# Relational graph layer with normalization on one core: base products read two chunks later, node sums three, masks made two chunks ahead

## The chip, the core and the metric

The kernel runs on one core of a Trainium2 chip. The core has five engines that run their own instruction streams and meet through semaphores: TensorE (matrix products, "PE" in the profile, with its weight loads as "PEld"), VectorE ("DVE"), ScalarE ("ACT"), GpSimd ("POOL") and SyncE ("SP"). Products of TensorE land in PSUM, which VectorE and ScalarE read; everything else lives in SBUF, and DMA queues move data between SBUF and device memory. The metric is the device time of one execution in microseconds (us); less is better.

## The reference

There are 50,000 nodes with 128 features, 850,000 edges sorted by their destination (400,000 in both directions and one from each node to itself), and 16 relations whose 128x128 matrices are mixtures of 8 bases. Two layers run one after the other, then a residual and a normalization of each node's row:

```python
def _rgcn_layer(h, src, dst, rel, basis, w_comp, loop_w, bias):
    W = jnp.einsum('rb,bio->rio', w_comp, basis)
    seg = dst.astype(jnp.int32) * N_REL + rel.astype(jnp.int32)
    agg = jax.ops.segment_sum(h[src], seg, num_segments=N_ENT * N_REL)
    agg = agg.reshape(N_ENT, N_REL, -1)
    msg = jnp.einsum('nri,rio->no', agg, W)
    out = msg + h @ loop_w + bias
    return jax.nn.relu(out)
...
x = _layernorm(x + _L0_gnn_ref(x, ...), axis=-1)
```

## The kernel before

**Chunks.** The 800,000 edges that are not from a node to itself are cut into 625 chunks (C) of 10 tiles (K) of 128 edges. Since the edges are sorted by destination, a tile touches few nodes; the kernel lets a tile touch at most 12 (WN). A chunk therefore has 120 "slots", 12 to a tile. Both layers go through all chunks, so there are 1,250 passes of the loop over `c`, fully unrolled.

**One chunk.** GpSimd gathers the source rows, one indirect DMA for each tile (`gather`, L198), into one of GATHERS = 6 buffers, in an order that is two chunks (FETCH) ahead in its own stream. VectorE makes the mask `hot` (L789): for each edge, base and slot, the weight of the edge's relation in that base, or 0. Ten products `pa` (L837, five in each half) sum the gathered rows by base and slot; ScalarE copies each half to `aT` (L844). `slots` multiplies `aT` by the eight bases (`ps`, L689, eight products into one sum), and ScalarE copies the result (L693). `nodes_of` puts slots at their nodes: a 0/1 mask `own` (L699) times the slots, and, because a node's edges can run over a chunk's end, a second mask `shift` (L706) times the last chunk's result `kept`, moved by the distance between the two chunks' first nodes; both products go into `pn` (L703, L707). VectorE adds what the node has from itself (`a`, L709), ScalarE copies `pn` to `kept` (L712), and the row is finished and stored.

**Edges from a node to itself** do not go through chunks. `from_itself` takes a block of 128 nodes: load (L656), transpose on TensorE into `po` (L205), copy to `hT` (L207), two products `hb` with four bases each (L667), each weighed by VectorE into `by` (L670), one product with the loop weights (L678), its bias (L679), a sum over nine parts (L681), and a store to `L` (L682). Every eighth block also needs `loop_weights` (L642, L646). 391 blocks in a layer go with 625 chunks, about 62 blocks for 100 chunks.

**Order.** The orders of TensorE and GpSimd are those in which the program is written (`manual_schedule`); those of the other engines are left to the framework's scheduler. TensorE works through its instructions in order, so one that waits holds up all that follow. In pass `c` its order is: `pn` of chunk c-2, transpose of the block, `pa` first half, `hb` first, `ps` of chunk c-1, `hb` second, `pa` second half, the block's loop product, and every fourth chunk the relation weights `pm` (L615). The mask for chunk c+1 is made at the end of the pass.

**PSUM.** It has eight banks, and each has a user: `fixed` (constants and scratch of VectorE), two for `pa`, one for `po` (transposes, loop products, set-up), one for `ps`, one for `pn`, one for `pm`, one for `hb`.

Of the kernel before, what the change touches and what calls it, by code (L numbers as in the profile page):

```python
# [48 lines left out]
P = 128  # L50
EPR = 850000
ROW = 10
WN = 12
# [13 lines left out]
GATHERS = 6  # L67
# [9 lines left out]
def tile_rgcn_resnorm(  # L77
# [57 lines left out]
    grid, apart = fixed[:, 0, :], fixed[:, 1, :]  # L135
    nc.vector.tensor_copy(grid, col)
    nc.vector.tensor_scalar(apart, col, -1.0, part, op0=OP.mult, op1=OP.add)
# [57 lines left out]
    ps_h = ctx.enter_context(tc.tile_pool(name="ps_h", bufs=1, space=PSUM))  # L195
# [22 lines left out]

    base_i = consts.tile([1, C], I32, name="base_i")
    dist = consts.tile([P, C], F32, name="dist")  # L220
    slot = consts.tile([P, C], F32, name="slot")
    first_of = consts.tile([1, C], F32, name="first_of")
# [6 lines left out]
    picked = consts.tile([P, 5 * NG + len(ROWS) + 3], F32, name="picked")  # L229
    ones = consts.tile([P, max(LIVE, C)], F32, name="ones")  # L230
    place = consts.tile([P, RUN], F32, name="place")
    place64 = consts.tile([P, LIVE], F32, name="place64")
# [12 lines left out]
    nc.gpsimd.iota(place64, pattern=[[64, LIVE]], base=0, channel_multiplier=0, allow_small_or_imprecise_dtypes=True)  # L245
# [190 lines left out]
    def rows_of(j, pool):  # L436
# [44 lines left out]
        if (r0 + m) * LIVE > M:  # L481
            last = pool.tile([P, 1], F32, name="last")
            nc.vector.tensor_scalar(
                last, part, -64.0 * LIVE, 64.0 * (M - 1 - r0 * LIVE), op0=OP.mult, op1=OP.add
            )
            nc.vector.scalar_tensor_tensor(
                keyf[:m], place64[:m], last[:m], keyf[:m], op0=OP.subtract, op1=OP.max
            )
        rel8 = pool.tile([P, LIVE], U8, name="rel8")
# [27 lines left out]
        nc.vector.tensor_copy(dist[:, a:b], po[:, : b - a])  # L517
# [13 lines left out]
    def count_up(pool):  # L531
# [22 lines left out]
        nc.vector.tensor_scalar(picked[0:1, last + 2 :], first_of[:, 0:1], 0.0, None, op0=OP.is_equal)  # L554
# [8 lines left out]
            off[:, 1:2], total[:1, 1:2], float(E + 2 * NG * (P + 1) + 2 * C + 1), None, op0=OP.not_equal  # L563
# [19 lines left out]
    def chunked():  # L583
        with (
# [3 lines left out]
        ):  # L588

# [34 lines left out]
            def loop_weights(i, n):  # L624
# [15 lines left out]
                po = ps_o.tile([P, D], F32, name="po")  # L640
# [8 lines left out]
            def from_itself(i, of, n, lws):  # L649
# [11 lines left out]
                hT = turned(h[:m], m, sb)  # L661
                by = sb.tile([P, NB + 1, D], F32, name="by", bufs=1)
                few = BANK // D
                for b in range(0, NB, few):
                    yield
                    hb = ps_h.tile([P, BANK], F32, name="hb")
                    nc.tensor.matmul(  # L667
                        hb[:m], hT, BASIS[n][:, b : b + few, :].rearrange("p b d -> p (b d)"), start=True, stop=True
                    )
                    nc.vector.tensor_tensor(  # L670
                        by[:m, b : b + few, :],
                        hb[:m].rearrange("p (b d) -> p b d", d=D),
                        lw[:m, b : b + few, None].to_broadcast([m, few, D]),
                        op=OP.mult,
                    )
                yield
                po = ps_o.tile([P, D], F32, name="po")
# [7 lines left out]
            def slots(c, k, aT, n):  # L685

                ps = ps_n.tile([P, D], F32, name="ps")
# [4 lines left out]
                st = sb.tile([P, D], F32, name="slots")  # L692
# [3 lines left out]
            def nodes_of(kept, c, k, st, n0, ls, xw, n):  # L696

                own = sb.tile([P, P], F32, name="own")
                nc.vector.tensor_scalar(  # L699
                    own[: k * WN], grid[: k * WN, :P], slot[: k * WN, c : c + 1], None, op0=OP.is_equal  # L700
                )
                pn = ps_n.tile([P, D], F32, name="pn")
                nc.tensor.matmul(pn, own[: k * WN], st[: k * WN], start=True, stop=not c)  # L703
                if c:
                    shift = sb.tile([P, P], F32, name="shift")
                    nc.vector.tensor_scalar(shift, apart, dist[:, c - 1 : c], None, op0=OP.is_equal)  # L706
                    nc.tensor.matmul(pn, shift, kept, start=False, stop=True)  # L707
                a = sb.tile([P, D], F32, name="a")
                nc.vector.tensor_add(a, pn, ls)  # L709
                if c < C - 1:  # L710
                    kept = sb.tile([P, D], F32, name="kept")
                    nc.scalar.copy(kept, pn)  # L712
# [8 lines left out]
                return kept  # L721
# [48 lines left out]
            for n, of in enumerate((x, H1)):  # L770

                kept, summed_up, multiplied, lws = None, None, None, []
                base, ks = [at(0), None, None], lambda c: min(K, -(-M // P) - c * K)
                own_parts = []
# [5 lines left out]
                def hot_of(c, pm):  # L780
# [7 lines left out]
                    hot = hp.tile([P, K, NB, WN], F32, name="hot")  # L788
# [8 lines left out]
                def loaded(n0):  # L797

                    ls = sb.tile([P, D], F32, name="ls_of")
# [5 lines left out]
                    return ls, xw  # L805
# [3 lines left out]
                for c in range(C):  # L809
                    now[0] = c  # L810
                    if n == 0 and c:

                        next(coming, None)
                        while ready[0] + 1 < len(ROWS) and 2 * min(C, c + FETCH + 4) > ROWS[ready[0] + 1]:
                            next(coming)
                    if c:
                        base = [at(c)] + base[:2]
# [4 lines left out]
                    if c == 0:  # L822
# [3 lines left out]
                        hot = hot_of(c, pm)  # L826
                    if c > 1:
                        kept = nodes_of(kept, c - 2, ks(c - 2), summed_up, base[2], *others, n)
                        others = loaded(base[1])
                    parts = own_parts[0] if own_parts else iter(())  # L830
                    next(parts, None)
                    aT = hp.tile([P, NB, S], F32, name="aT")
                    for k in range(0, ks(c), PER):
# [14 lines left out]
                        if k == 0:  # L848
                            next(parts, None)
                            if c:  # L850
                                summed_up = slots(c - 1, ks(c - 1), multiplied, n)
                            next(parts, None)
                    multiplied = aT
                    for parts in own_parts:
                        done(parts)
                    if c == 1:
                        others = loaded(base[1])
                    if c + 1 < C:
                        if (c + 1) % Q == 0:
                            pm = next(weigh)  # L860
                        hot = hot_of(c + 1, pm)
                        if c + 2 < C and (c + 2) % Q == 0:
                            weigh = weights(c + 2, n)
                            next(weigh)
                        own_parts = []
                        for i in own_nodes(c + 1):
                            own_parts.append(from_itself(i, of, n, lws))
                            if len(own_parts) == 1:
                                next(own_parts[0])
# [5 lines left out]
                last = loaded(base[0])  # L875
                kept = nodes_of(kept, C - 2, ks(C - 2), summed_up, base[1], *others, n)
                summed_up = slots(C - 1, ks(C - 1), multiplied, n)
                nodes_of(kept, C - 1, ks(C - 1), summed_up, base[0], *last, n)
            ordered.close()

    def summed():
        L1 = dram.tile([N, D], F32, name="L1")
        L2 = dram.tile([N, D], F32, name="L2")
        with tc.tile_pool(name="io", bufs=2) as io, tc.tile_pool(name="sbf", bufs=2) as sb:
# [28 lines left out]
            def looped(h, n, L, m, n0):  # L913

                op = ps_n.tile([P, D], F32, name="pn")
# [30 lines left out]
            def added(h, n, L):  # L946


                def block(r0, p):
# [13 lines left out]
                    for e in range(ROW):  # L963
# [35 lines left out]
                        op = ps_n.tile([P, D], F32, name="pn")  # L999
# [68 lines left out]
```

## Time and profile before

| | |
|---|---|
| median of 3 runs (lowest to highest) | 18,924.72 us (18,904.69 to 18,941.53) |
| the profiled execution | 18,936.72 us |
| its span, first to last instruction | 18,934.8 us |
| mean granted TensorE clock | 0.72 |
| busy: TensorE / its weight loads | 10,703.0 / 9,174.1 us |
| busy: VectorE / ScalarE / GpSimd | 6,595.5 / 2,775.4 / 11,864.7 us |
| the span over 1,250 chunks | 15.1 us |

A row of the profile names line, engine and operation, what is written and read, how often, busy time, the mean of one in ns, and the idle time of the engine just before, with what ended most of it. "issue" means that nothing which the profile shows was waited for, and "remote" that the semaphore came but its sender could not be told. The ends of matrix products are modelled, not observed; when a product is really done is seen by when its reader, waiting for it, begins. An indirect DMA on GpSimd is shown for the time in which its descriptors are made, and its data come later.

### The profile page before, as it was taken

How to read it: one execution, taken by the hardware profiler on the slowest of the kernel's cores; microseconds unless marked ns; L12 is line 12 of the kernel's file. 1: busy time of each engine (PE TensorE's matmuls, PEld its weight loads, DVE VectorE, ACT ScalarE, POOL GpSimd, SP SyncE). 2: the span in 40 equal slices, each digit the busy share in tenths (PEclk: the TensorE clock that was granted, in tenths of full speed). 3: DMA queues.
4: the chain of work that ended last, by engine and by line, in shares of the span. 5: the costliest groups of instructions: out<-in, count | busy, mean ns of one | idle time of the engine just before them, and what ended most of it. 6: DMA issues, size and time to landing. Idle time of an engine off the chain costs nothing.

```text
span 18934.8 us, 187693 instructions
## 1 busy us (share of the span) xinstructions
PE 10703.0 (57%) x59198; PEld 9174.1 (48%) x59198; DVE 6595.5 (35%) x14269; ACT 2775.4 (15%) x7815; POOL 11864.7 (63%) x12533
## 2 busy tenths in 40 slices
PE   4555555555555555555555555555555555555555
PEld 3444445444544445445445555445454444444445
DVE  4333334333333332333223333333333333333333
ACT  1111111111111111111111111111111111111111
POOL 5666666665666666666656666666666666666665
PEclk7777777676777776777767777777777777777777
DMA  2222222222222222222222222222222222222222
GB/s 80 69 69 65 68 66 66 66 66 63 62 62 61 61 61 61 61 61 61 61 55 66 67 66 67 66 66 67 65 66 66 66 66 66 65 66 66 66 65 62
DMA packets 1164943, 1227.02 MB, mean 65 GB/s; under 512 B 283055, under 2 KB 952401, under 8 KB 1163937
## 3 DMA queue, kind: packets, MB, share of 16 engines
q0 software_dynamic: 403552, 826.82, 16.8%
q1 hardware_dynamic: 757169, 386.65, 7.1%
q8 instruction: 472, 7.73, 0.2%
q14 instruction: 534, 4.37, 0.1%
q10 hardware_dynamic: 3216, 1.45, 0.0%
HBM read 1059.55 MB, written 154.23 MB: 64 GB/s over the span
## 4 chain that ended last, share of the span: by engine, by line
another core or an unknown queue 22%; PE 17%; issue 7%; DVE 5%; ACT 2%; DMA 0%; POOL 0%; SPq 0%; ACTq 0%; DVEq 0%; POOLq 0%
PE pa L837 6%; PE ps L689 4%; PE hb L667 4%; DVE ls L681 1%; DVE by L670 1%; DVE hot L789 1%; PE pn L703 1%; ACT aT L844 1%; PE pn L707 1%; PE po L678 0%; PE po L205 0%; DVE by L679 0%; ACT slots L693 0%; ACT sd L574 0%
## 5 line engine op out<-in xcount | busy, mean ns | idle before, releaser
L198 POOL DMA_INDIRECT g<-H,src x6250 | 5910.6, 946 | 3393.7 <-issue 1422.2
L198 POOL DMA_INDIRECT g<-in_x_dram,src x6250 | 5927.4, 948 | 3338.4 <-issue 1411.5
L837 PE MATMUL pa<-hot,g 128*128 128x96 f32 x25000 | 4125.3, 326 | 1898.8 <-DVE hot L789 1388.2
L837 PEld LDWEIGHTS pa<-hot,g 128*128 128x128 f32 x25000 | 4014.2, 243 | 2402.1 <-DVE hot L789 1434.6
L689 PEld LDWEIGHTS ps<-basis,aT 128*120 128x120 f32 x20000 | 3222.4, 240 | 927.1 <-issue 849.3
L667 PE MATMUL hb<-basis,hT 128*128 128x512 f32 x3128 | 2273.3, 818 | 2107.1 <-ACT hT L207 915.7
L689 PE MATMUL ps<-basis,aT 128*120 128x128 f32 x20000 | 3211.3, 329 | 224.3 <-issue 150.5
L670 DVE TENSOR_TENSOR by<-hb,lw 128x512 f32<-128x512 f32 x1564 | 1080.1, 691 | 6152.1 <-remote 2557.6
L789 DVE TENSOR_TENSOR hot<-pm,own 128x960 f32<-128x960 f32 x1250 | 1432.6, 1153 | 4113.1 <-remote 3585.2
L844 ACT COPY aT<-pa 128x480 f32<-128x480 f32 x2500 | 1395.2, 558 | 6619.3 <-remote 3577.7
L703 PE MATMUL pn<-slots,own 120*128 120x128 f32 x2500 | 708.5, 373 | 2448.5 <-ACT slots L693 1502.1
L703 PEld LDWEIGHTS pn<-slots,own 120*128 120x128 f32 x2500 | 470.3, 235 | 2593.2 <-ACT slots L693 1583.3
L667 PEld LDWEIGHTS hb<-basis,hT 128*128 128x128 f32 x3128 | 638.1, 253 | 2191.4 <-ACT hT L207 943.1
L681 DVE TENSOR_REDUCE ls<-by 128x128 f32<-128x1152 f32 (+1 forms) x782 | 1656.9, 2119 | 12.1
L693 ACT COPY slots<-ps 120x128 f32<-120x128 f32 x1250 | 332.4, 266 | 5771.4 <-remote 3733.1
L205 PE MATMUL po<-ident,h_own 128*128 128x128 f32 (+1 forms) x782 | 295.8, 378 | 1151.9 <-issue 399.5
L205 PEld LDWEIGHTS po<-ident,h_own 128*128 128x128 f32 (+1 forms) x782 | 138.1, 177 | 1219.9 <-issue 415.1
L707 PE MATMUL pn<-kept,shift 128*128 128x128 f32 x2496 | 604.8, 332 | 12.1 <-DVE shift L706 6.3
L615 PE MATMUL pm<-each,is_rel 128*128 128x64 f32 x3140 | 438.6, 281 | 114.4 <-issue 110.4
L707 PEld LDWEIGHTS pn<-kept,shift 128*128 128x128 f32 x2496 | 493.7, 245 | 14.2 <-DVE shift L706 7.7
L712 ACT COPY kept<-pn 128x128 f32<-128x128 f32 x1248 | 336.1, 269 | 1079.7 <-DVE a L709 603.5
L709 DVE TENSOR_TENSOR a<-pn,ls_of 128x128 f32<-128x128 f32 x1250 | 355.1, 284 | 386.6 <-remote 133.1
(148 smaller groups left out, 5082.0 us busy)
## 6 DMA issues: line engine op xcount, KB each, us to landing
g<-in_x_dram,src POOLq DMA_INDIRECT x6250
g<-H,src POOLq DMA_INDIRECT x6250
ls_of<-L SPq DMA_DIRECT2D x1250, 64.0 KB
L<-ls SPq DMA_DIRECT2D x780, 64.0 KB
H<-h SPq DMA_DIRECT2D x625, 64.0 KB
xw<-in_x_dram SPq DMA_DIRECT2D x625, 64.0 KB
out_dram<-o SPq DMA_DIRECT2D x625, 64.0 KB
h_own<-in_x_dram SPq DMA_DIRECT2D x390, 64.0 KB
```

Of the source, the lines that this page charges most:

```text
L198: nc.gpsimd.indirect_dma_start(out=to, out_offset=None, in_=of, in_offset=bass.IndirectOffsetOnAxis(ap=idx, axis=0))
L205: nc.tensor.transpose(tp[:, :m], h, ident[:m, :m])
L615: nc.tensor.matmul(of[:, :, j * NB : (j + 1) * NB], is_rel[:m, j * P : (j + 1) * P], EACH[n][:m], start=True, stop=True,)
L667: nc.tensor.matmul(hb[:m], hT, BASIS[n][:, b : b + few, :].rearrange("p b d -> p (b d)"), start=True, stop=True)
L670: nc.vector.tensor_tensor(by[:m, b : b + few, :], hb[:m].rearrange("p (b d) -> p b d", d=D), lw[:m, b : b + few, None].to_broadcast([m, fe ...
L681: nc.vector.tensor_reduce(ls[:m], by[:m].rearrange("p b d -> p d b"), AX.X, OP.add)
L689: nc.tensor.matmul(ps[: k * WN], aT[:, b, : k * WN], BASIS[n][:, b, :], start=b == 0, stop=b == NB - 1)
L703: nc.tensor.matmul(pn, own[: k * WN], st[: k * WN], start=True, stop=not c)
L707: nc.tensor.matmul(pn, shift, kept, start=False, stop=True)
L789: nc.vector.tensor_tensor(hot[:, : ks(c)], pm[:, c % Q * K : c % Q * K + ks(c), :, None].to_broadcast([P, ks(c), NB, WN]), own[:, : ks(c), ...
L837: nc.tensor.matmul(pa[:, i * NB * WN : (i + 1) * NB * WN], g[:, k + i, :], hot[:, k + i].rearrange("e b w -> e (b w)"), start=True, stop=True,
L844: nc.scalar.copy(aT[:, :, k * WN : (k + m) * WN].rearrange("d b (i w) -> d i b w", w=WN), pa[:, : m * NB * WN].rearrange("d (i b w) -> d i ...
```

## The change

- **Node sums lie three chunks back** and nothing is kept from chunk to chunk. `pn` of chunk c-3 is made at the end of pass `c` from two slot results: its own, and that of the chunk before it, placed by a second mask of the same kind (`next_slot`). `shift`, `apart`, `dist`, `kept` and its copy go. The slot results have 5 buffers.
- **Bases lie two chunks back**: `ps` of chunk c-2 is made in pass `c`; `aT` has 3 buffers.
- **Masks are made two chunks ahead**: `hot` of chunk c+2 at the end of pass `c`, with 3 buffers.
- **A node block spreads over two passes**: its transpose at the start of pass `c`, its `hb` products and loop product in pass c+1, in the places in which they stood in pass `c`. Its rows are loaded two chunks ahead.
- **PSUM**: `hb` gets two banks. To pay for it, `ps`, `pn`, the loop product and the loop weights become four quarters of one tile, `sums`, that is allocated once and fills one bank; transposes keep `po`.
- **Gather buffers**: 5 for 6.
- A few counts that guard the assumptions change with it.

```diff
-GATHERS = 6
+GATHERS = 5
...
-    ps_h = ctx.enter_context(tc.tile_pool(name="ps_h", bufs=1, space=PSUM))
+    ps_h = ctx.enter_context(tc.tile_pool(name="ps_h", bufs=2, space=PSUM))
+
+    sums = ps_n.tile([P, BANK // P, P], F32, name="sums")
...
-        nc.vector.tensor_copy(dist[:, a:b], po[:, : b - a])
+        nc.vector.tensor_tensor(next_slot[:S, a:b], slot[:S, a:b], po[:S, : b - a], op=OP.subtract)
...
-                po = ps_o.tile([P, D], F32, name="po")
+                po = sums[:, 3, :]
                 for h in range(2):
                     nc.tensor.matmul(
                         po[:, : AT * NB], is_rel[:m, h, :], EACH[n][:m], start=h == 0, stop=h == 1
...
                 hT = turned(h[:m], m, sb)
+                yield
                 by = sb.tile([P, NB + 1, D], F32, name="by", bufs=1)
                 few = BANK // D
                 for b in range(0, NB, few):
-                    yield
                     hb = ps_h.tile([P, BANK], F32, name="hb")
...
-                yield
-                po = ps_o.tile([P, D], F32, name="po")
+                    yield
+                po = sums[:, 2, :]
                 nc.tensor.matmul(po[:m], hT, LOOP[n], start=True, stop=True)
                 nc.vector.tensor_add(by[:m, NB, :], po[:m], BIAS[n][:m])
...
-                ps = ps_n.tile([P, D], F32, name="ps")
+                ps = sums[:, 0, :]
...
-                st = sb.tile([P, D], F32, name="slots")
+                st = sb.tile([P, D], F32, name="slots", bufs=5)
...
-                pn = ps_n.tile([P, D], F32, name="pn")
-                nc.tensor.matmul(pn, own[: k * WN], st[: k * WN], start=True, stop=not c)
-                if c:
-                    shift = sb.tile([P, P], F32, name="shift")
-                    nc.vector.tensor_scalar(shift, apart, dist[:, c - 1 : c], None, op0=OP.is_equal)
-                    nc.tensor.matmul(pn, shift, kept, start=False, stop=True)
+                looked = [(c, slot[:, c : c + 1])]
                 if c:
+                    looked.append((c - 1, next_slot[:, c - 1 : c]))
...
+                pn = sums[:, 1, :]
+                for j, (i, at_node) in enumerate(looked):
+                    k = ks(i) * WN
+                    own = sb.tile([P, P], F32, name=f"own{j % 2}")
+                    nc.vector.tensor_scalar(own[:k], grid[:k, :P], at_node[:k], None, op0=OP.is_equal)
+                    nc.tensor.matmul(pn, own[:k], st[i][:k], start=j == 0, stop=j == len(looked) - 1)
                 a = sb.tile([P, D], F32, name="a")
                 nc.vector.tensor_add(a, pn, ls)
-                if c < C - 1:
-                    kept = sb.tile([P, D], F32, name="kept")
-                    nc.scalar.copy(kept, pn)
...
                     if c > 1:
-                        kept = nodes_of(kept, c - 2, ks(c - 2), summed_up, base[2], *others, n)
-                        others = loaded(base[1])
-                    parts = own_parts[0] if own_parts else iter(())
-                    next(parts, None)
-                    aT = hp.tile([P, NB, S], F32, name="aT")
+                        loaded(c - 2)
+
+                    own, one = coming_own.pop(c, []), iter(())
+                    if len(own) == 1:
+                        one = own[0]
+                        next(one, None)
+                    hot = hots.pop(c)
+                    aT = aTs[c] = hp.tile([P, NB, S], F32, name="aT", bufs=3)
...
                         if k == 0:
-                            next(parts, None)
-                            if c:
-                                summed_up = slots(c - 1, ks(c - 1), multiplied, n)
-                            next(parts, None)
+                            next(staged, None)
+                            if c > 1:
+                                sum_up(c - 2)
...
-                    for parts in own_parts:
-                        done(parts)
...
+                    done(staged)
...
+                    staged = one
+                    if c > 2:
+                        finish(c - 3)
+                    if c + 2 < C:
+                        if (c + 2) % Q == 0:
                             pm = next(weigh)
-                        hot = hot_of(c + 1, pm)
...
+                        hots[c + 2] = hot_of(c + 2, pm)
...
+                    for to in [c + 1] if c == 0 else [2, 3] if c == 1 else [c + 2]:
+                        if to < C:
+                            coming_own[to] = [from_itself(i, of, n, lws) for i in own_nodes(to)]
```

Here `sum_up(c)` calls `slots`, and `finish(c)` calls `nodes_of`. In pass `c` TensorE's order is now: transpose of this chunk's block, `pa` first half, first `hb` of the last chunk's block, `ps` of chunk c-2, `pa` second half, second `hb`, the loop product, `pn` of chunk c-3, and every fourth chunk `pm`.

## The prediction

> **What bounds the kernel now.** First the busy shares: no engine is full, GpSimd is busiest. Then its rows among the costliest groups, the first two lines below: 12,500 gathers of 0.947 us, 11,838 us in all, with 6,732 us idle before them. The list of GpSimd's waits splits that idle time.
>
> ```profile
> PE 10703.0 (57%) x59198; PEld 9174.1 (48%) x59198; DVE 6595.5 (35%) x14269; ACT 2775.4 (15%) x7815; POOL 11864.7 (63%) x12533
> ...
> L198 POOL DMA_INDIRECT g<-H,src x6250 | 5910.6, 946 | 3393.7 <-issue 1422.2
> L198 POOL DMA_INDIRECT g<-in_x_dram,src x6250 | 5927.4, 948 | 3338.4 <-issue 1411.5
> ```
> ```profile
> POOL g L198 <- issue: 2833.6, 9114, 5.8
> POOL g L198 <- PE pa L837: 1621.8, 1277, 33.9
> POOL g L198 <- remote: 1586.1, 1153, 8.9
> ```
>
> The 9,114 short gaps are 0.31 us, GpSimd's own rhythm (0.30 in the timeline). So the gathers cannot take less than 11,838 + 12,500 x 0.30 = 15,588 us. What is left, 6,732 - 3,750 = 2,982 us, is GpSimd standing, mostly for `pa`: a buffer is free when TensorE has used it. The last 365 us of the 18,935 are start, tail and the rest. In the trace's starts of gathers, 1,671 runs are parted by over 1.4 us between starts: 1.34 stops for each of 1,250 chunks, 2,982 / 1,671 = 1.78 us each.
>
> Why does GpSimd stand, if TensorE is 57% busy? The timeline of one chunk answers:
>
> ```profile
> 14066.53 0.56 ACT L844 COPY aT<-pa 128x480 f32<-128x480 f32 x1 [7.26 <-issue]
> 14066.53 1.16 DVE L789 TENSOR_TENSOR hot<-pm,own 128x960 f32<-128x960 f32 x1 [9.76 <-issue]
> ...
> 14069.14 0.94 POOL L198 DMA_INDIRECT g<-H,src  x1 [0.30 <-issue]
> 14070.73 0.35 DVE L699 TENSOR_SCALAR own<-fixed,slot 120x128 f32<-120x128 f32 x1 [2.64 <-remote]
> 14072.83 0.35 DVE L706 TENSOR_SCALAR shift<-fixed,dist 128x128 f32<-128x128 f32 x1 [1.75 <-remote]
> ...
> 14072.86 0.27 ACT L207 COPY hT<-po 128x128 f32<-128x128 f32 x1 [5.78 <-remote]
> 14073.13 0.56 ACT L844 COPY aT<-pa 128x480 f32<-128x480 f32 x1
> 14073.14 0.94 POOL L198 DMA_INDIRECT g<-H,src  x1 [3.06 <-remote]
> 14073.18 0.50 PEld L667 LDWEIGHTS hb<-basis,hT 128*128 128x128 f32 x2 [10.78 <-ACT hT L207]
> ```
>
> The transpose behind that `hT` has its modelled end at 14,060.56, its reader starts at 14,072.86. The products were issued and done by the model, but word of them came 10 us late, and then for all at once, 2 to 3 us after GpSimd had stopped. That is the rule over the whole trace: of TensorE's recorded semaphore updates, some 0.5 a microsecond come within 1.3 us of a gather's start, 10.5 in the slice 3.0 to 3.25 us after the last one. In the first 4 us after gathers resume, readers of `aT` mostly begin 0.1 us after their product; later in a run they take 4 to 12 us. So the kernel beats: GpSimd runs about a chunk of gathers, its credits run out, it stops, word of the products comes, TensorE gets on, credits flow. **The time is 12.47 us of gathers a chunk plus its stops**, and what counts is how far TensorE can issue without word of its own products: each `pa` issued before a stop is a credit at the stop.
>
> TensorE's waits show where it stands:
>
> ```profile
> PE pn L703 <- ACT slots L693: 1502.1, 357, 22.5
> PE pa L837 <- DVE hot L789: 1388.2, 177, 42.4
> PE hb L667 <- ACT hT L207: 915.7, 126, 12.2
> ...
> PE hb L667 <- DVE by L670: 515.7, 86, 29.3
> ...
> PE po L205 <- DVE by L679: 329.2, 135, 13.4
> ```
>
> **What the distances remove.** In their groups with "issue" and the rest, these cost: `pn` 2,448 us, `pa` 1,899, `hb` 2,107, the transpose 1,152; 7,606 us or 6.1 us a chunk. After the change `pn` reads slots of the pass before, `pa` a mask a pass old, `hb` a transpose of the pass before and has two banks; the transpose's bank is no longer the loop product's. All four waits as they stand lose their cause.
>
> **What it leaves alone.** `own` for `shift` is the same on VectorE (339 for 337 ns) and on TensorE (a second `pn` product of 373 ns for one of 332; 1,248 x 2 instructions x 0.041 = 102 us of busy time on an engine with 8,200 idle). The copy to `kept` (336 us of ScalarE's 2,775) goes, hidden and worth nothing while ScalarE is 15% busy. Masks, loads and stores are the same in number. Five buffers for six: GpSimd ends a chunk's gathers a median 70 us, 4.6 chunks, before they are used; one chunk less leaves 55, which hides a landing. The cover is gone only where gathers are held up for longer than that; single waits of over 55 us are few (TensorE's longest are 42.7 us for `hot` and 62.5 without a cause shown). Nothing, with 100 us as the other end. Guards and set-up: under 5 us. Each layer's tail has two more sums behind the last `pa`, some 5 us each with their readers, 20 us in all; layer 2's first gather waits behind it (37.2 us once now).
>
> **SP.** `h_own` is loaded a chunk earlier into three buffers, so its wait for the old transpose (5,486 us at L656 now, `remote`, `pa` and `po` together) stands a chunk nearer to the transpose that frees it, and behind it in SP's queue stand loads of `ls_of` and stores of rows. `ls_of` has a whole chunk to land before `a` needs it. Between nothing and 1 us a chunk if `a` is late; I take nothing.
>
> **What it adds: one bank for four.** `ps`, `pn`, the loop product and the loop weights are now quarters of `sums`. If quarters count as independent there is no new wait. The row for that is the old `po` bank: where transposes and loop products used the same bytes, TensorE waited for L679 (1,152 us with its neighbours). No row shows two users of different bytes in one bank. Here a rule of the Trainium skill speaks against the change: "PSUM — Partial Sum Buffer", section "PSUM bank collisions raise a hardware error", says that an engine may not read a bank while TensorE writes to it, even in other columns, and that one has to guard by bank, not by address. A framework that follows it makes TensorE's every write to `sums` wait for all earlier readers of the bank. In the new order these are three waits:
> - `ps` behind `a` (pn of the pass before), at a distance of a transpose, five `pa` and one `hb`. Nearest row: `hb` behind `hT`, at five `pa`: (2,107 - 516) / 780 = 2.0 us. A further `hb` lies between, but VectorE may be in its 2.1 us sum (L681): 1.75 us a chunk.
> - the loop product behind the copy of `ps`, at five `pa` and one `hb`. Rows: `hb` behind `by` at sixteen `ps` instructions, 516 / 780 = 0.66, and 2.0 as above: 1.3 us, for 62% of chunks 0.8.
> - `pn` behind L679, with nothing between. Row: the transpose behind L679, 1.47 us with `pn` between (0.8 us): 2.3 us for 62%, 1.4; in the other chunks `pn` behind the copy of `ps`, 2.0 for 38%, 0.7.
>
> By the row the added wait is 0; by the rule 1.75 + 0.8 + 2.1 = 4.7 us of the 6.1 come back. I take the rule. More important is where they come back: the wait that parts one beat from the next, slots' copy between `ps` and the next product, was in front of `pn` and is now in front of the loop product, at the same distance. So by the rule TensorE gains no second chunk between stops.
>
> **The sum.** What still goes are stops in mid-chunk. Two waits, `hT` and `by`, stood between the halves of `pa`, so that a stop often found only half a chunk issued; now one, for `a`, stands there. Of the 0.34 stops a chunk beyond one I leave a third, 0.11 (both ends: none, and all 0.34). 1,250 x 1.10 x 1.78 = 2,450 us of standing for 2,982: 530 us less, 20 of it back in the tails, and 18,935 becomes some 18,420. The profiled execution took 18,936.7 us, 2 more than its span and 12 more than the median of the runs, so **18,410 us**, 2.7% faster. With none or all of the 0.34 left: 18,180 to 18,930.
>
> **Rivals.**
> - A, **the distances work in full**: quarters are independent, or the waits on the bank fall into the prompt stretch. TensorE then issues 1.5 to 2 chunks between stops: 1,250 / 1.75 x 1.78 = 1,270 us of standing, 17,220 us. For it: `aT` readers in the first 4 us of a run take 0.1 us. Against: the rule, and `pn` directly behind L679.
> - B, **slower: `pn` behind L679**. The loop product is now the last thing before `pn`, and word of it comes behind five `pa` and one `hb`[...]. Where that falls late in a run of gathers, TensorE stands before the next chunk's first `pa`, and a stop frees nothing new: another stop of 1.78 us. It outweighs the gain from 298 of the 780 blocks on (530 / 1.78); at 60% of them it costs 833 us: 19,240. For it: late in a run readers wait 4 to 12 us. Against: the loop product is released at the stop itself and should be done in the 4 prompt us.
> - C, **nothing changes**: the beat is set by gathers and word of products alone, one stop and a third as before; 18,930.
>
> **Numbers.** My forecast has 0.40, A 0.18, B 0.34, C 0.08. Within 0.2% is what a measurement of this kernel can tell from no change (its three runs span 0.2%): faster 0.57, same 0.07, slower 0.36. The forecast's own range is 18,180 to 18,750. The range for eight in ten reaches to A's 17,220 and past B's 19,240: 17,150 to 19,500.
>
> **What would show it.** Right: `pn` no longer waits for slots, `pa` not for `hot`, `hb` not for `hT`; instead `ps` waits for `a`, the loop product for slots, `pn` for L679; runs of gathers between stops grow from 7.5 to about 9. A is right if those bank waits are missing and runs reach 15 or more. B is right if `pn` stands for L679 over 1,500 us and runs shorten. The prediction is wrong at its root if the stops vanish and TensorE's products still report late, or if readers take no 10 us even in long runs: then gathers do not hold up the reports.

## The result and the profile after

The changed kernel takes 18,726.98 us, median of four runs (18,704.36 to 18,737.19), beside 18,923.88 for the kernel before, measured with it: a ratio of **0.9895, interval 0.9877 to 0.9912**. It is faster, as forecast, but by 1.05% and not by 2.7%. The profiled execution's span is 18,735.4 us, 199.4 less than before.

First the page after: its busy shares, and the rows of the gathers and of the three users of the shared bank `sums` (instructions | busy, mean ns | idle before, what ended most of it).

```profile
PE 11303.9 (60%) x59202; PEld 9682.0 (52%) x59202; DVE 6635.0 (35%) x14275; ACT 2537.0 (14%) x6567; POOL 11856.0 (63%) x12532
...
L200 POOL DMA_INDIRECT g<-in_x_dram,src x6250 | 5919.9, 947 | 3352.7 <-issue 1428.9
L200 POOL DMA_INDIRECT g<-H,src x6250 | 5910.7, 946 | 3346.0 <-issue 1439.6
...
L731 PE MATMUL sums<-slots,own 120*128 120x128 f32 x5000 | 1327.9, 412 | 4360.9 <-DVE by L702 1356.0
...
L712 PE MATMUL sums<-basis,aT 128*120 128x128 f32 x20000 | 3241.2, 330 | 729.6 <-issue 514.2
...
L701 PE MATMUL sums<-loop,hT 128*128 128x128 f32 x1564 | 438.5, 370 | 1613.4 <-ACT slots L716 1275.2
```

The gathers' idle time has hardly moved: 6,698.7 us for 6,732. So most of the 199 us did not come from the stops that the prediction counted. TensorE's waits (us in total, times, longest) have changed places as it said:

```profile
PE sums L731 <- DVE by L702: 1356.0, 455, 23.7
PE sums L701 <- ACT slots L716: 1275.2, 330, 18.3
PE sums L731 <- issue: 1268.8, 240, 16.3
PE sums L731 <- ACT slots L716: 1230.3, 248, 26.7
PE sums L712 <- issue: 514.2, 216, 25.1
...
PE sums L712 <- DVE a L733: 184.9, 84, 7.4
```

The wait of `pa` for `hot` is gone, and that of `hb` for `hT` is down from 915.7 us to 47.9. In their place `pn` (L731) stands for L702, which only shares its bank, and the loop product (L701) for the copy of `ps`. One such place in the timeline (start, duration, engine, instruction, idle before):

```profile
14003.53 0.49 PE L701 MATMUL sums<-loop,hT 128*128 128x128 f32 x2 [1.34 <-ACT slots L716]
14004.50 0.94 POOL L200 DMA_INDIRECT g<-H,src  x1 [0.30 <-issue]
...
14011.20 0.94 POOL L200 DMA_INDIRECT g<-H,src  x1 [0.78 <-remote]
...
14014.47 0.29 DVE L702 TENSOR_TENSOR by<-sums,bias 128x128 f32<-128x128 f32 x1 [0.69 <-remote]
...
14014.82 1.22 PE L731 MATMUL sums<-slots,own 120*128 120x128 f32 x4 [10.80 <-DVE by L702]
...
14016.04 2.29 PE L866 MATMUL pa<-hot,g 128*128 128x96 f32 x10
...
14016.90 0.94 POOL L200 DMA_INDIRECT g<-H,src  x1 [4.75 <-PE pa L866]
```

The loop product goes out at 14,003.53, its reader L702 begins 11 us later, 2.3 us after GpSimd's last gather ended. Then `pn` and ten `pa` go out within 4 us and GpSimd is let on. The beat of before is still there.

The place also shows a firmer sign of a wait than the label in the list: L731 starts 0.06 us after L702 has ended (14,014.47 + 0.29). I counted by that sign: an idle stretch of TensorE "ends on a reader" if TensorE starts again 35 to 75 ns after an instruction of VectorE or ScalarE has ended. Of the 7,411 us for which TensorE stands idle in this trace, 7,044 end on a reader (before: 7,951 of 8,212). L731 alone stands 2,981 us for L702, in 770 places; the list gives 1,356 to it and puts much of the rest down to "issue" or to other engines.

**Where the 199 us came from.** I took every gap between the starts of two gathers above 1.4 us and split off those in which GpSimd does something else in between. It does so 19 times, all in layer 1: it stores parts of the index tables for later chunks (`FULL`, `LREL`), which VectorE prepares bit by bit between its other work. The stores stand at fixed places among the gathers, and GpSimd waits there until VectorE has the input. Their rows among GpSimd's instructions, before:

```profile
L428 POOL DMA_INDIRECT LREL<-l_rel,l_to x10 | 12.2, 1216 | 93.6 <-DVE l_rel L420 72.9 <-DVE loops L337 20.4 <-issue 0.3
L372 POOL DMA_INDIRECT FULL<-full,to_i x10 | 11.5, 1150 | 201.8 <-DVE shift L706 103.2 <-DVE full L370 56.3 <-DVE own L699 42.3
```

and after:

```profile
L374 POOL DMA_INDIRECT FULL<-full,to_i x10 | 11.5, 1149 | 119.1 <-DVE full L372 119.1
L430 POOL DMA_INDIRECT LREL<-l_rel,l_to x10 | 11.5, 1145 | 21.8 <-DVE l_rel L422 19.3 <-issue 2.1 <-DMA g<-in_x_dram,src 0.3
```

The idle time before these twenty (the first lies ahead of all gathers) fell from 295.4 us to 140.9. The whole account, over the rhythm of 1.2485 us from gather to gather (the gap between the layers counts as a stop):

```
                                     before   after
stops between two gathers, number     1,652   1,558
  their time, us                      2,939   2,898     -41
19 gaps that hold a table store, us     294     141    -153
rhythm, start, end, us               15,702  15,696      -6
```

Three quarters of the gain lie in a place that the prediction did not look at, and the stops it was about gave 41 us.

### The profile page after: what moved, and what is told of

Same layout as the page of the kernel before. It is cut to its first block, busy times and chain, and to the rows that moved or that the text cites. A ratio compares the mean times of both kernels' runs of the same rounds, so it can differ in the third digit from the quotient of the medians.

```text
span 18735.4 us, 188402 instructions
## 1 busy us (share of the span) xinstructions
PE 11303.9 (60%) x59202; PEld 9682.0 (52%) x59202; DVE 6635.0 (35%) x14275; ACT 2537.0 (14%) x6567; POOL 11856.0 (63%) x12532
## 5 line engine op out<-in xcount | busy, mean ns | idle before, releaser
L731 PE MATMUL sums<-slots,own 120*128 120x128 f32 x5000 | 1327.9, 412 | 4360.9 <-DVE by L702 1356.0
L712 PEld LDWEIGHTS sums<-basis,aT 128*120 128x120 f32 x20000 | 3188.5, 240 | 1451.3 <-issue 1107.4
L712 PE MATMUL sums<-basis,aT 128*120 128x128 f32 x20000 | 3241.2, 330 | 729.6 <-issue 514.2
L731 PEld LDWEIGHTS sums<-slots,own 120*128 120x128 f32 x5000 | 1008.6, 283 | 4601.1 <-DVE by L702 1468.7
L701 PEld LDWEIGHTS sums<-loop,hT 128*128 128x128 f32 x1564 | 314.8, 234 | 2197.9 <-ACT slots L716 1592.9
L701 PE MATMUL sums<-loop,hT 128*128 128x128 f32 x1564 | 438.5, 370 | 1613.4 <-ACT slots L716 1275.2
L716 ACT COPY slots<-sums 120x128 f32<-120x128 f32 x1250 | 330.7, 265 | 5238.2 <-remote 3725.7
L733 DVE TENSOR_TENSOR a<-sums,ls_of 128x128 f32<-128x128 f32 x1250 | 356.3, 285 | 1532.0 <-remote 442.7
L730 DVE TENSOR_SCALAR own<-fixed,slot 120x128 f32<-120x128 f32 x1250 | 425.5, 340 | 1160.4 <-PE sums L731 740.0
L638 PEld LDWEIGHTS pm<-each,is_rel 128*128 128x128 f32 x3140 | 615.9, 294 | 3.5 <-DVE is_rel L633 3.3
```

Source lines behind the costliest of these rows:

```text
L638: nc.tensor.matmul(of[:, :, j * NB : (j + 1) * NB], is_rel[:m, j * P : (j + 1) * P], EACH[n][:m], start=True, stop=True,)
L701: nc.tensor.matmul(po[:m], hT, LOOP[n], start=True, stop=True)
L712: nc.tensor.matmul(ps[: k * WN], aT[:, b, : k * WN], BASIS[n][:, b, :], start=b == 0, stop=b == NB - 1)
L730: nc.vector.tensor_scalar(own[:k], grid[:k, :P], at_node[:k], None, op0=OP.is_equal)
L731: nc.tensor.matmul(pn, own[:k], st[i][:k], start=j == 0, stop=j == len(looked) - 1)
```

## The experiments

The theory after this result: while GpSimd makes gathers, TensorE itself is held up, not only the word of its products (the semaphore that tells a reader that a product is done), so its throughput within a run of gathers sets the beat, and distance between product and reader buys little. The rivals: it is the word alone, and the shared bank hides the gain of the distances; or the traffic of the gathered rows holds TensorE up.

### Without gathers, uncoupled, and with plain loads (e1 to e4)

e1 and e2 gather only the first passes:

```diff
-                        for k in range(ks(to)):
+                        for k in range(ks(to)) if n * C + to < GATHERS else ():
```

> The kernel before, but only the first six chunks are gathered; all later chunks multiply what lies in the six buffers, so the node sums are of wrong rows. Theory (gathers hold up the word of TensorE's products): with no gathers, readers begin within 0.5 us of their product everywhere, TensorE's waits shrink to short ones, and the time is TensorE's own chain, 9 to 12 ms. Rival (the chain of product, reader, next product is simply that long, and GpSimd only follows it): the waits for slots, hT and hot stay at several us each, and the time stays over 16 ms.

> The same cut in the changed kernel (first five chunks gathered). Theory: 8 to 11 ms, and below the kernel before with the same cut by at least 5%, since the distances hide short latencies even where long ones remain exposed by the shared bank. Rival: over 16 ms. If it is no faster than the kernel before with the same cut, the shared bank gives back in full what the distances win, with or without gathers.

e1 took 8,974.31 us and e2 9,132.58, where the kernel before took 18,947.9 on the same chip (one run of each). Without gathers the change costs 1.8%, and the waits of TensorE in e2 say for what:

```profile
PE sums L731 <- DVE by L702: 674.8, 766, 21.2
PE sums L712 <- DVE a L733: 177.7, 312, 5.5
```

TensorE is 90% busy in e1, so half of the usual time is not its own work, though the granted clock differs too (0.95 in e1, 0.72 in the kernel before).

e3 lets TensorE multiply a constant tile, so that gathers never wait for it:

```diff
+    still = consts.tile([P, K, D], F32, name="still")
+    nc.vector.memset(still, 0.125)
...
-                    g = rows[(n * C + c) % GATHERS]
+                    g = still
```

> The changed kernel with all its gathers, but TensorE multiplies a constant tile instead of the gathered rows (the sums are of constants), so no gather waits for TensorE and TensorE waits for no gather; four buffers. Theory: GpSimd never stops inside a layer, runs through its 6,250 gathers at 1.25 us each (7.8 ms a layer), and meanwhile word of the products stays slow, so TensorE does at most half of the layer's chunks in that time and the rest after it: over 19 ms although two waits were taken away. Rival (the wait for buffers is a plain cost): GpSimd's 15.6 ms or TensorE's chain set the time, 15.6 to 17 ms.

It took 25,459.32 us. Two stretches of its span, the first with gathers end to end, the second after the last gather (stretch, length, then busy time and instructions of PE, PEld, DVE, ACT, POOL; granted clock, DMA share, GB/s):

```profile
14000.00:20000.00 6000.00, 615.07 (x2170) 490.99 (x2171) 250.65 (x588) 101.34 (x257) 4589.02 (x4285) 0.51 0.17 49
23500.00:25000.00 1500.00, 1345.04 (x10012) 1179.79 (x10012) 1096.60 (x2723) 475.50 (x1210) 0.00 (x0) 0.99 0.16 45
```

2,170 / 6,000 = 0.36 matrix instructions a microsecond under gathers, 10,012 / 1,500 = 6.67 without: a factor of 18. The granted clock (0.51 for 0.99) explains two of the 18. What TensorE waited for in the first stretch:

```profile
PE sums L733 <- issue: 2126.6, 46, 59.7
PE sums L703 <- issue: 1511.0, 28, 54.2
PE sums L714 <- issue: 695.5, 101, 36.4
PE pa L868 <- issue: 683.7, 309, 3.9
PE sums L714 <- DVE a L735: 173.5, 5, 35.0
```

"issue" means that the profile shows nothing it waited for; with two smaller rows it makes 5,240 of the 5,413 us listed. Here the label misleads. One of the longest waits, from the timeline:

```profile
15018.93 1.09 POOL L200 DMA_INDIRECT g<-H,src  x1 [0.30 <-issue]
15019.35 0.27 ACT L718 COPY slots<-sums 120x128 f32<-120x128 f32 x1 [42.81 <-remote]
...
15019.67 0.80 PE L703 MATMUL sums<-loop,hT 128*128 128x128 f32 x2 [53.92 <-issue]
```

L703 writes the bank that the copy L718 reads, and starts 0.05 us after the copy has ended; the copy had stood 42.8 us, while gathers ran on. All 93 idle stretches over 10 us in this window end on a reader, and so do 4,454 of the 5,413 us. So TensorE is mostly seen waiting for readers, and the readers for word. Only the remaining 959 us, in stretches of mostly some 2.5 us, are TensorE held up with no reader behind it. e3 shows that gathers make word late even where nothing waits for their data; that TensorE itself is what is slow, it does not show.

e4 brings the same bytes with plain loads from SyncE, from other rows of the table:

```diff
-                            gather(rows[(n * C + to) % GATHERS][:, k, :], of, src[:, to * K + k : to * K + k + 1])
+                            first = (to * K + k) * 7 % (N // P) * P
+                            nc.sync.dma_start(rows[(n * C + to) % GATHERS][:, k, :], of[first : first + P, :])
```

> The changed kernel with each gather replaced by a plain load of 128 rows in a block, issued by SP: the same bytes into the same buffers with the same waits, other rows (wrong sums), no descriptors made on GpSimd. Theory, form 1 (descriptors on GpSimd hold up the reports): as without gathers, 9 to 12 ms, unless SP's issue (10 more loads of some 0.35 us a chunk) stands in the way. Form 2 (the data or their landing signals hold up the reports): readers still take 4 to 12 us late in a run of loads, time over 15 ms.

10,879.02 us, with GpSimd idle. So neither the number of bytes nor the buffers hold TensorE up, but something in the way in which GpSimd gathers. e4 changes three things at once: who makes the descriptors, the queue that moves the data, and which rows are read. It does not tell which of them it is.

How late word is can be read from the copies to `aT`: the time from the modelled end of the last `pa` of a half to the start of its copy, 2,500 in each trace.

```
                                    median us   share over 4 us
before                                   1.03             37%
after                                    2.95             41%
own banks (e6, below)                    6.65             74%
before, no gathers (e1)                  0.09            0.2%
after, plain loads (e4)                  0.04            0.0%
```

### Own banks, and five buffers alone (e5 to e7)

e5 is a control that frees two banks (the constants in `fixed` go to SBUF, `hb` has one bank, `slots` four buffers); e6 uses them to end the sharing.

```diff
+    sums_n = ps_n.tile([P, BANK // P, P], F32, name="sums_n")
+    sums_o = ps_n.tile([P, BANK // P, P], F32, name="sums_o")
...
-                po = sums[:, 2, :]
+                po = sums_o[:, 2, :]
...
-                pn = sums[:, 1, :]
+                pn = sums_n[:, 1, :]
```

> Control for the next kernel: the changed kernel with the constants of `fixed` in SBUF instead of PSUM, one bank for hb instead of two, four buffers for slots instead of five; sums still shared. Both theories: near the changed kernel (0.99 of before), at most 1% worse because hb waits for by again.

> As the control, but ps, pn and the loop product have a bank each (loop weights share with the loop product). Theory (the shared bank gives the distances back): the waits of pn for L702, of the loop product for slots and of ps for a vanish; TensorE can then issue a second chunk before it needs word, runs of gathers between stops reach 15 and more, time 0.91 to 0.96 of before. Rival (one stop a chunk is set by the gathers and the credits, whatever TensorE may issue): runs stay at 10, time 0.98 to 1.0.

Beside the kernel before (19,040.2 us on that chip) e5 gave 0.9905 (0.9888 to 0.9921), 18,866.88 us, and e6 **0.9724 (0.9708 to 0.974)**, 18,521.78 us. So the shared bank costs 1.8%, and with it gone the distances work as written. But the stops do not become fewer: 1,727 in e6 for 1,717 in e5, only shorter, 1.60 us for 1.81. The commonest run is still exactly ten gathers, 717 of 1,747. What TensorE does late in a run is in e6's timeline:

```profile
14017.28 0.32 PE L865 MATMUL pa<-hot,g 128*128 128x96 f32 x1 [1.15 <-issue]
14017.80 0.94 POOL L199 DMA_INDIRECT g<-H,src  x1 [0.30 <-issue]
...
14017.99 0.52 PE L865 MATMUL pa<-hot,g 128*128 128x96 f32 x1 [0.39 <-issue]
14018.70 0.32 PE L865 MATMUL pa<-hot,g 128*128 128x96 f32 x1 [0.20 <-issue]
...
14019.40 0.32 PE L865 MATMUL pa<-hot,g 128*128 128x96 f32 x1 [0.38 <-issue]
...
14020.13 0.50 PE L865 MATMUL pa<-hot,g 128*128 128x96 f32 x1 [0.41 <-issue]
...
14020.82 1.16 PE L865 MATMUL pa<-hot,g 128*128 128x96 f32 x4 [0.18 <-issue]
...
14021.08 0.95 POOL L199 DMA_INDIRECT g<-H,src  x1 [2.34 <-PE pa L865]
```

`pa` products that wait for nothing go out one by one, 0.70 us apart, for 1.4 us beyond the end of GpSimd's last gather (14,018.74) too; its last data packet ends at 14,019.91, and from 14,020.82 four go out at once. So the stretch could belong to the making of descriptors or to the moving of the data. In e6's list of waits these products, and those of `ps` (L711), stand first and third; the second line is the price of the one bank that `hb` has left:

```profile
PE pa L865 <- issue: 2394.7, 3168, 3.7
PE hb L689 <- DVE by L692: 1252.7, 403, 13.2
PE sums L711 <- issue: 1174.3, 1500, 4.0
```

Here the label holds: of the 6,642 us for which TensorE stands idle in e6, 4,112 end on no reader; in e5 it was 203 of 7,466. So it takes own banks to see TensorE itself held up; with the shared bank it stands for readers first.

e7 is the kernel before with `GATHERS = 5` for 6.

> The kernel before with five gather buffers instead of six, nothing else. My prediction: nothing (within 0.3%), since a chunk's gathers end 70 us before use and one chunk less leaves 55. Rival (the sixth buffer carries the beat through uneven chunks): 1 to 3% slower, and then the change's distances won that much more than its result shows.

0.9944 (0.9928 to 0.9961): one buffer fewer makes the kernel before faster by 0.56%, half of what the whole change brings. In its trace the 19 gaps with a table store hold 145 us, as after the change (141), for 294 before. From the last gather of a chunk to its first `pa` it is a median 70.3 us before, 55.5 in e7 and 56.3 after. The stores have a fixed place among the gathers, so the further GpSimd runs ahead of the other engines, the longer it must wait there for VectorE, which follows TensorE. That reading fits these numbers, but it is not shown: the stores were not moved to test it, the trace of before is from another chip than that of e7, and in e5 and e6, with five buffers too, the same 19 gaps hold only 44 and 45 us. So the number of buffers is not all that sets them.

### Half of the bases, and four buffers (e8 to e11, f1 to f4)

e8 and f2 are e6, and e9 is the kernel before, with eight products a chunk fewer; e10 and f3 are the kernel before, e11 and f4 are e6, with `GATHERS = 4`; f1 is the changed kernel as it is.

```diff
-                for b in range(NB):
+                for b in range(0, NB, 2):
```

> The own-banks version, with every second base left out of the sum ps (8 of its products per chunk are not computed, so the messages hold half of the bases). Theory, TensorE's throughput while gathers run sets the beat: the left-out products were issued at about 0.7 us and more each late in a run of gathers, so taking some 8 of 47 products a chunk away shortens the catch-up: ratio to the kernel before 0.90 to 0.95, against 0.972 with all bases; the mean run of gathers grows above 8. Rival, distance from product to reader (the word of a product, not its execution): the distances are the same, so 0.967 to 0.975, runs of 7 as in the own-banks version.

> The kernel before with the same cut: every second base left out of the sum ps, 8 products a chunk fewer, all waits from product to reader as before. Theory, TensorE's throughput under gathers: falls too, ratio 0.93 to 0.98. Rival, distance alone: the readers of pn, pa and hb wait as before, ratio 0.995 to 1.005.

> The kernel before with 4 gather buffers for 6. Five buffers gave 0.994. Theory, fewer buffers let GpSimd run less far into the stretch in which TensorE is slowed, and stop and restart sooner: 0.985 to 0.995. Rival, five was only a better fit to the 5 gathers of a half chunk: at four it turns round, 1.00 to 1.02.

> The own-banks version with 4 gather buffers for 5. Theory, fewer buffers, shorter runs into the slowed stretch: 0.96 to 0.972, below the own-banks version. Rival, the buffers hide part of the stop: 0.975 to 0.99.

> The changed kernel as it is. On a chip where the kernel before takes about 18.9 ms and GpSimd stops about 1.3 times a chunk: 0.987 to 0.992, as at first. On a chip where it takes 15.8 ms, with 12,500 gathers at 1.26 us end to end as on the last one: 0.998 to 1.004, since the rows of GpSimd are the whole time and TensorE has waits to spare.

> The own-banks version with every second base left out of ps (half of the messages' bases are not computed, 8 products a chunk fewer), for a chip where the kernel before takes about 18.9 ms. Theory, TensorE's throughput while gathers run sets the beat: 0.90 to 0.95, against 0.972 with all bases, mean run of gathers above 8. Rival, distance from product to reader alone: 0.967 to 0.975, runs of 7. On a chip of the 15.8 ms kind: 0.998 to 1.002 again, which tells nothing between them.

> The kernel before with 4 gather buffers for 6, for a chip where the kernel before takes about 18.9 ms; five gave 0.994. Theory, fewer buffers let GpSimd run less far into the stretch in which TensorE is slowed: 0.985 to 0.995. Rival, five was only a better fit to the five gathers of a half chunk: 1.00 to 1.02. On a chip of the 15.8 ms kind 1.000.

> The own-banks version with 4 gather buffers for 5, for a chip where the kernel before takes about 18.9 ms. Theory, fewer buffers, shorter runs into the slowed stretch: 0.96 to 0.972. Rival, the buffers hide part of the stop: 0.975 to 0.99. On a chip of the 15.8 ms kind 1.001.

These eight fell on two chips where the kernel before takes 15,809.59 and 15,806.76 us, a sixth less than on the chips of e1 to e7:

```
e8   1.0002 (0.9993 to 1.0012)   f1   1.0003 (0.9993 to 1.0012)
e9   0.9985 (0.9975 to 0.9994)   f2   1.0002 (0.9992 to 1.0012)
e10  1.0000 (0.9990 to 1.0009)   f3   1.0002 (0.9992 to 1.0011)
e11  1.0014 (1.0004 to 1.0023)   f4   1.0016 (1.0007 to 1.0026)
```

f1 is the same program as the kernel after, on such a chip. Its page (the same columns as above), and below it one stretch of 1,500 us:

```profile
PE 11455.6 (72%) x59202; PEld 9289.4 (59%) x59202; DVE 6549.2 (41%) x14275; ACT 2579.0 (16%) x6567; POOL 11891.6 (75%) x12532
...
L200 POOL DMA_INDIRECT g<-in_x_dram,src x6250 | 5944.9, 951 | 1934.9 <-issue 1148.7
L200 POOL DMA_INDIRECT g<-H,src x6250 | 5921.4, 947 | 1940.0 <-issue 1164.5
...
L731 PE MATMUL sums<-slots,own 120*128 120x128 f32 x5000 | 943.2, 316 | 1095.6 <-DVE by L702 1090.0
```
```profile
14000.00:15500.00 1500.00, 1124.56 (x5649) 902.04 (x5650) 623.01 (x1537) 265.91 (x682) 1135.18 (x1198) 0.78 0.30 78
```

A gather takes as long as before (947 to 951 ns), but GpSimd hardly stands: 100 us in 151 stops, and 15,755 us from the first gather's start to the last one's end, 12,500 x 1.26. TensorE starts 5,649 / 1,500 = 3.77 matrix instructions a microsecond under gathers end to end, all that it has to do (59,202 in 15,817 us); e3 had 0.36. Word comes at once: the copies to `aT` begin a median 0.04 us after their last product, 0.2% of them over 4 us. The wait for L702 is still there, 1,090 us, and costs nothing.

Counted in the traces, the starts of matrix instructions a microsecond while gathers run, by the time since the run of gathers began:

```
us since the run's start   0-2   2-4   4-6   6-8  8-10  10-12.5  later
before                    3.55  4.38  5.01  4.25  3.29     1.31   0.40
after                     3.35  4.17  4.30  4.44  3.12     1.79   0.81
own banks (e6)            3.47  4.15  5.45  4.48  2.20     1.41   0.82
after, on f1's chip       3.63  3.26  3.72  3.47  3.16     4.05   3.78
```

On the first kind of chip TensorE fades after some 8 us of a run, whatever the kernel; on the second it does not. On the second the time is the gathers' own, so half of the bases, other banks or other numbers of buffers have next to nothing to shorten (e9 gains 0.15%, e11 and f4 lose 0.14% and 0.16%; unexplained), and e8 to f4 cannot tell throughput from distance. **Left open**: half of the bases and four buffers on a chip of the first kind; e6 itself on one of the second; whether the two kinds are a property of the chips or of their condition at the time; what of a gather does it, its descriptors or its data; and whether products whose word comes late were done late, or only reported late.

## Why the prediction was right in direction and wrong in size

- **The gathers' floor** of 15,588 us held. The rhythm makes 15,612 us in the trace after, and on the second kind of chip the floor, 15,755, is nearly the whole time (15,817).
- **The removed waits** went as named, and **the bank rule** was the right choice over the row that said 0. The three groups on `sums` now stand idle for (4,361 + 1,613 + 730) / 1,250 = 5.4 us a chunk; 4.7 were forecast. By parts: `pn` 3.5 for 2.1, the loop product 1.3 for 0.8, `ps` behind `a` 0.6 for 1.75. The largest error is `pn` behind L679 (now L702): 2.4 us a chunk for 1.4. The framework guards all of `sums`, which fits the guard by bank that the Trainium skill's "PSUM — Partial Sum Buffer" (section "PSUM bank collisions raise a hardware error") asks for; e6 against e5 puts the price at 1.8% of the time. The quarters are slices of one tile, so no run here parts a guard by bank from one by tile.
- **The step that failed is the sum: "Of the 0.34 stops a chunk beyond one I leave a third", at 1.78 us each, -530 us.** Measured over stops between gathers: 1.32 a chunk before, 1.25 after, and each dearer, 1.86 us for 1.78; -41 us. Runs of gathers grew from 7.5 to 7.9, not to 9. (The sum also has 1.10 where its own third makes 1.11, which is 22 us.) The reason given was that "a stop often found only half a chunk issued". For each stop the traces tell whether the `pa` products that last read the tile to be filled had started before GpSimd's last gather ended:

```
                                          before   after     e6
stops                                      1,648   1,553   1,713
  products already started                 1,261   1,285   1,682
of these in mid-chunk (sixth gather)         737     639     646
  products already started                   544     637     646
```

  Only 193 of the 737 mid-chunk stops before were of the kind that the prediction wanted to remove. The change did remove them, down to 2, but those in which the products had started and word was missing rose from 544 to 637.
- **Behind it lies the premise "what counts is how far TensorE can issue without word of its own products: each `pa` issued before a stop is a credit at the stop".** That word is late was right: e1 and e4 take the gathers away and the lateness goes. But GpSimd goes on at the word and not at the issue, and at 1,285 of 1,553 stops after the change the products had already been issued. In e6, which issues further ahead, it is 1,682 of 1,713, its word is later still (6.65 us), and it has no fewer stops than e5. Distance helps by shortening a stop (1.81 to 1.60 us in e6), not by sparing it. Why GpSimd stops where it does, most often after ten gathers, stays open.
- **Five buffers at "nothing, with 100 us as the other end"** had the wrong sign: about 0.56% of gain (e7). My cover argument asked only who needs the buffer, and not what stands in GpSimd's own stream behind it: the table stores, which were among its waits (`FULL`, `LREL`) and stood for 295 us. That they are where e7 gains is argued, not shown.
- **The tails** at +20 us were too dear: from the last gather's end to the end of the span 39.3 us for 41.9, between the layers' gathers 38.9 for 38.8. **SP**, costed at nothing, shows nothing: its longest wait is still the load of `h_own`, 4,712 us in its three largest parts for 5,486.
- **The rivals.** A (17,220, the distances in full) falls even with own banks: 18,522. B (`pn` behind L679, now L702, 19,240): the wait came, 1,356 us by the list and 2,981 by what ended it, against a mark of 1,500, and e6 shows what it takes; but it was paid for by what went, and runs did not shorten. C (nothing changes) is nearest by the stops alone: without the 19 gaps the gain would have been some 46 us, 0.24%.

## What to carry to other kernels

When an engine's products are "late", find out before distance is added to its loop whether what its readers wait for has been issued already: if it has, issuing further ahead spares no wait. A low count of instructions per microsecond does not tell a slow engine from one that waits; look at what ended each idle stretch, also where the profile says "issue". Of an engine that runs ahead on buffers, list everything in its stream: the further ahead it is, the longer it may stand at each instruction whose input comes from the engines behind it, and a buffer fewer can be a gain. Run the kernel before on more than one chip before a gain of 1% is taken as the kernel's: here it was 1.05% on one kind and none on the other (0.03% slower, between 0.07% faster and 0.12% slower).

## What the hardware showed that was not expected

- While GpSimd made indirect gathers end to end, TensorE started 0.36 matrix instructions a microsecond for 6.67 without (e3), mostly because readers got word of issued products late, here by over 40 us. In e6, where fewer readers stand in the way, products that wait for nothing go out in steps of 0.7 us late in a run. Gathers were slower too in that stretch of e3 (1.40 us from one to the next for 1.25). The same number of bytes by plain loads (e4) left the whole kernel at 10,879 us for 18,727.
- Two of the chips showed none of it: 3.77 instructions a microsecond under gathers end to end, word a median 0.04 us behind the product (f1), and 15,785 to 15,832 us for every version. The granted clock does not explain it (0.78 in f1, 0.72 after).
- As this framework guards a shared PSUM bank, it costs by who reads it, not by which columns: 766 waits for L702 in e2, with no gathers but the first.
